# Attention weights made from a second product of keys and queries instead of by transposing, in an attention and mixture-of-experts layer

## The chip, the cores and the metric

The kernel runs on one core of a Trainium2 chip. The metric is the time of one execution on the device in microseconds (us), lower is better. A core has five engines with queues of their own, each executing in order: TensorE (PE, with its weight loads listed as PEld), VectorE (DVE), ScalarE (ACT), GpSimd (POOL) and SyncE (SP), which here only issues DMAs. Matmul results lie in PSUM, which has eight banks of 512 fp32 values for each of 128 partitions.

## The reference

All data is fp32. x is 8 batches x 512 tokens x 256 features.

```python
qkv = x @ w_qkv                       # 16 heads of 16 features
q = q / sqrt(16)
scores = where(causal, q @ k.T, NEG)  # per batch and head, 512 x 512
x = layernorm(x + (softmax(scores) @ v) @ w_out)

probs = softmax(x @ gate_w.T)         # 16 experts
idx = top_k(probs + gate_b, 6)        # the six best for each token
y = sum over chosen e of probs[e] * ((silu(x @ W1.T + B1) * (x @ W3.T + B3)) @ W2.T + B2)   # hidden 176
z = the same form without a gate, hidden 352, for every token (shared expert)
x = layernorm(x + y + z)
```

## The kernel before

**Attention.** A batch's tokens are four blocks of 128 (NT = 4). The 16 heads are eight pairs; heads are reached as m (0 or 1, the half of the features), s (0 or 1, which head of a pair) and r (0 to 3, the group of 32 partitions), so one (m, s) stands for four heads. `transpose_x` brings x to features on partitions, `project_qk` and `project_v` project. Queries are stored once for each s, with the rows of the pair's other head set to zero (`par` holds the parity masks), so that a matmul over 32 partitions gives one head's scores. v is stored in `v2` with 16 columns of ones between the heads, so that the product with v also gives the sum of the weights.

A step is (q, m, s): a block of queries against all keys before it.
- `scores` (L348) makes four matmuls, one for each r, each into a one-bank tile `sc` (the pool ps_s has four such banks). For each, DVE adds the causal mask, scales by -0.25 and takes the minimum in one custom instruction (L368), and POOL forms minimum minus that (L378), that is, the scaled score less its maximum, in `e`.
- `turn_weights` (L384) transposes the 128 x 128 blocks of `e` on PE into a bank of `ps` (L390), and ACT takes the exponential out of it (L392) into `eT`.
- `weighted_v` (L396) multiplies `eT` with v into `po`, whose four r lie in four groups of 32 output columns.
- `normalize` (L407) runs once for each (q, m): ACT and DVE merge the two s, and DVE divides by the sum.

Steps are software-pipelined: unit i holds the scores of step i, the transposes of step i-1 and the product with v of step i-2. There are 16 steps and 18 units a batch.

**Tokens.** After a query block, `later` queues `finish_tokens` (output projection `pr`, residual, norm), `transpose_tokens`, `gate`, `place` and three `send` for it. `gate` and `place` find the six experts of each token and the slots for its row; `send` scatters the rows with indirect DMAs from POOL (L543) to a list of the group in DRAM, `xs`. `shared_units` computes the shared expert of a batch while the next batch's attention runs.

**Experts.** Batches are gathered in GROUPS. When the last row of a group is sent, `table` and `spread` make a list of tiles of 128 rows of one expert. For each tile `expert_units` fetches rows (`xg`, on SP's queue), transposes them (L780) and the hidden layer of an earlier tile (L784), and makes the up product `pab` (L799, bias matmul L806) and the down product `py` (L826); POOL scatters the result to `ys` (L835). `combine_units` loads each token's six rows, sums them with their weights (L893), normalises and stores. A group has 24 tiles for each batch and 15 more: 63, 111 and 63.

**Order.** PE's order is written out by hand (`tc.manual_schedule`); the other engines' queues are ordered by the framework's scheduler. `line` is the list of attention units; `put` spreads the expert units of a group between the units after its last row is sent, until the next group is ready. The units of the last group, and the combine units of the one before among them, run after attention; the combine of the last group runs at the very end, alone. PSUM: four banks ps_s, one ps_o, three ps. In the last group every second tile bank is taken from ps_s.

Of the kernel before, what the change touches and what calls it, by code (L numbers as in the profile page):

```python
# [19 lines left out]
P = 128  # L20
# [3 lines left out]
HD = 16  # L24
TOP_K = 6
NOWHERE = 1 << 20
GROUPS = (2, 4, 2)
# [4 lines left out]
def attn_moe_postln_kernel(  # L32
# [47 lines left out]
    ten = ctx.enter_context(tc.tile_pool(name="ten", bufs=8))  # L80
    dram = ctx.enter_context(tc.tile_pool(name="dram", bufs=1, space=DRAM))
    ps_s = ctx.enter_context(tc.tile_pool(name="ps_s", bufs=4, space=PSUM))
    ps_o = ctx.enter_context(tc.tile_pool(name="ps_o", bufs=1, space=PSUM))
    ps = ctx.enter_context(tc.tile_pool(name="ps", bufs=3, space=PSUM))

# [3 lines left out]
    def load_x(b):  # L89
        t = two.tile([P, NT, E + D], F32, tag="x", name=f"x_{b}")  # L90
        nc.sync.dma_start(out=t[:, :, E:], in_=x[b].rearrange("(t p) d -> p t d", p=P))
        xts[b] = t
# [27 lines left out]
    load_x(1)  # L120

# [19 lines left out]
    none = const.tile([P, E + S], F32, name="none")  # L141
    mask = none[:, E:]
    nc.gpsimd.memset(mask[:, : S - P], 0.0)

    nc.vector.memset(none[:, :E].bitcast(I32), NOWHERE)
    make_causal_mask(nc, mask[:, S - P :], NEG)
# [4 lines left out]
    )  # L151

# [65 lines left out]
    def split_biases():  # L218
# [7 lines left out]
        rest = ten.tile([E, 2, EH], F32, tag="eT", name="rest")  # L226
# [61 lines left out]
    for i in range(2):  # L288
        t = const.tile([P, 3, E], F32, tag=f"vals{i}", name=f"vals{i}")
        nc.gpsimd.tensor_copy(t[:, 1, :], eio)  # L290
        vals.append(t)

    cw = const.tile([P, P], F32, name="cw")
    nc.gpsimd.memset(cw, 0.0)
    nc.gpsimd.memset(cw[:, E : E + 1], 1.0)

    def attention(b):
# [12 lines left out]
        def project_qk(m):  # L310
            xT = st["xT"]
            if m == 0:
                st["qT"] = one.tile([P, ND, 2, S], F32, tag="qT", name=f"qT_{b}")
                st["kT"] = one.tile([P, ND, S], F32, tag="kT", name=f"kT_{b}")
            qT, kT = st["qT"], st["kT"]
            for w in range(2):
# [9 lines left out]
                if w == 0:  # L326
                    nc.scalar.mul(qT[:, m, 0, :], pr, par[:, 0:1])
                    nc.vector.tensor_scalar_mul(qT[:, m, 1, :], pr, par[:, 1:2])
                else:
                    nc.scalar.copy(kT[:, m, :], pr)  # L330
# [17 lines left out]
        def scores(q, m, s):  # L348

            n = (q + 1) * P  # L350
            qT, kT = st["qT"], st["kT"]
            es = []
            nb = four.tile([P, 4], F32, tag="nb", name=f"nb_{b}_{q}_{m}_{s}")
            scs = []
            for r in range(4):
                sc = ps_s.tile([P, S], F32, tag="sc", name=f"sc_{b}_{q}_{m}_{s}_{r}")
                nc.tensor.matmul(  # L357
                    sc[:, :n],
                    lhsT=qT[ts(r, 32), m, s, ts(q, P)],
                    rhs=kT[ts(r, 32), m, :n],  # L360
                    start=True,
                    stop=True,
                )
                scs.append(sc)
            for r in range(4):
                e = eight.tile([P, S], F32, tag="e", name=f"e_{b}_{q}_{m}_{s}_{r}")

                nc.vector.tensor_tensor_reduce(  # L368
                    out=e[:, :n],
                    in0=scs[r][:, :n],  # L370
                    in1=mask[:, S - n :],
                    scale=-0.25,
                    scalar=BIG,
                    op0=ALU.add,
                    op1=ALU.min,
                    accum_out=nb[:, r : r + 1],
                )
                nc.gpsimd.tensor_scalar(  # L378
                    e[:, :n], e[:, :n], -1.0, nb[:, r : r + 1], ALU.mult, ALU.add
                )  # L380
                es.append(e)
            return es

        def turn_weights(q, m, s, es):  # L384

            eTs = []
            for k in range(q + 1):
                tp = ps.tile([P, S], F32, tag="ps", name=f"tp_{b}_{q}_{m}_{s}_{k}")
                for r in range(4):
                    nc.tensor.transpose(tp[:, ts(r, P)], es[r][:, ts(k, P)], ident)  # L390
                eT = ten.tile([P, S], F32, tag="eT", name=f"eT_{b}_{q}_{m}_{s}_{k}")
                nc.scalar.activation(eT, tp, AF.Exp)  # L392
                eTs.append(eT)
            return eTs

        def weighted_v(q, m, s, eTs, po):  # L396
            for k in range(q + 1):
                for r in range(4):
                    nc.tensor.matmul(  # L399
                        po[ts(r, 32), m, s, :],  # L400
                        lhsT=v2[:, k, 4 * m + r, s : s + 2, :].rearrange("p h i -> p (h i)"),
                        rhs=eTs[k][:, ts(r, P)],
                        start=(k == 0),
                        stop=(k == q),
                    )

        def normalize(q, m, po, aT):  # L407

            nm = f"{b}_{q}_{m}"
            po = po[:, m]  # L410
            t = []
            for i in range(2):
                a = two.tile([P, P], F32, tag=f"t{i}", name=f"t{i}_{nm}")
                nc.scalar.mul(a, po[:, i, :], par[:, 1:2])
                t.append(a)
            den = two.tile([P, P], F32, tag="den", name=f"den_{nm}")

            nc.vector.scalar_tensor_tensor(
                t[0], po[:, 1, :], par[:, 0:1], t[0], ALU.mult, ALU.add
            )  # L420
            nc.vector.stream_shuffle(den, t[0], SWAP)
            nc.vector.reciprocal(den, den)
            nc.vector.scalar_tensor_tensor(  # L423
                t[1], po[:, 0, :], par[:, 0:1], t[1], ALU.mult, ALU.add
            )
            nc.vector.tensor_mul(aT[:, m, :], t[1], den)

        def finish_tokens(t, aT):
            pr = ps.tile([P, D], F32, tag="ps", name=f"pr_{b}_{t}")
            for c in range(ND):  # L430
                nc.tensor.matmul(
                    pr,
                    lhsT=aT[:, c, :],
# [16 lines left out]
        def gate(t):  # L450
# [17 lines left out]
            v = vals[t % 2]  # L468
# [14 lines left out]
            rank = two.tile(shp, F32, tag="rank", name=f"rank_{nm}")  # L483
            nc.vector.tensor_reduce(rank, gt, AX.X, ALU.add)
            sel = two.tile(shp, F32, tag="sel", name=f"sel_{nm}")
            nc.vector.tensor_scalar(sel, rank, TOP_K - 0.5, None, ALU.is_lt)
            nc.vector.tensor_mul(cw[:, :E], sel, pb)
            st["gate", t] = rank, sel

        def place(t):  # L490

            nm = f"{b}_{t}"
            rank, sel = st.pop(("gate", t))
            v = vals[t % 2]
# [38 lines left out]
            idi = two.tile([P, TOP_K], I32, tag="idi", name=f"idi_{nm}")  # L533
# [22 lines left out]
        steps = [(q, m, s) for q in range(NT) for m in range(ND) for s in range(2)]  # L556
        done = {}

        def front(i):

            if i < len(steps):
                done[i] = scores(*steps[i])
            if 1 <= i <= len(steps):
                done[i - 1] = turn_weights(*steps[i - 1], done[i - 1])
# [467 lines left out]
```

## Time and profile before

| what | value |
|---|---|
| median of 11 runs | 1595.69 us (1593.44 to 1599.05) |
| the profiled execution | 1594.6 us, of which the span is 1592.9 us |
| mean granted TensorE clock | 0.936 |
| busy: PE, DVE, ACT, POOL | 1401.8, 849.2, 619.5, 814.2 us |
| transposes of the weights (L390) | 1280 matmuls, 200.9 us |
| subtraction on POOL (L378) | 512 instructions, 271.8 us |

A line of a group gives the source line, the engine and operation, the written and read tiles, the shape and the count; then busy time, mean duration in ns, and idle time of the engine ahead of it with what ended it. A line of a timeline has the start in us, the duration of the merged run, engine, line, operation, tiles and count. A line of a table by windows has the stretch, its length, each engine's busy time with the count of instructions, and at the end the granted clock (1.00 is full speed), the busy share of the DMA engines and GB/s. Matmuls overlap and their ends are modelled, so distances between starts tell more than durations. An fp32 matmul shows as two records, an fp32 transpose as one.

### The profile page before, as it was taken

How to read it: one execution, taken by the hardware profiler on the slowest of the kernel's cores; microseconds unless marked ns; L12 is line 12 of the kernel's file. 1: busy time of each engine (PE TensorE's matmuls, PEld its weight loads, DVE VectorE, ACT ScalarE, POOL GpSimd, SP SyncE). 2: the span in 40 equal slices, each digit the busy share in tenths (PEclk: the TensorE clock that was granted, in tenths of full speed). 3: DMA queues.
4: the chain of work that ended last, by engine and by line, in shares of the span. 5: the costliest groups of instructions: out<-in, count | busy, mean ns of one | idle time of the engine just before them, and what ended most of it. 6: DMA issues, size and time to landing. Idle time of an engine off the chain costs nothing.

```text
span 1592.9 us, 30354 instructions
## 1 busy us (share of the span) xinstructions
PE 1401.8 (88%) x9204; PEld 950.9 (60%) x9204; DVE 849.2 (53%) x3058; ACT 619.5 (39%) x1637; POOL 814.2 (51%) x1127
## 2 busy tenths in 40 slices
PE   7698998999998899899999899998998998889950
PEld 4464664665765567566656666666665666556730
DVE  4565756755655564566466634455443332774235
ACT  2243333343443334344343444444443443334520
POOL 4367566657465454746565446534645422443320
PEclk9897988998999999899999999999999999999985
DMA  9711112221121121212221325222243523785334
GB/s 263 208 43 43 49 37 94 62 66 62 57 69 56 45 63 52 73 41 68 76 88 56 110 82 147 78 86 78 75 121 109 159 69 85 229 237 147 96 89 132
DMA packets 147497, 151.37 MB, mean 95 GB/s; under 512 B 51215, under 2 KB 122499, under 8 KB 147338
## 3 DMA queue, kind: packets, MB, share of 16 engines
q1 hardware_dynamic: 126474, 96.69, 22.3%
q0 software_dynamic: 20592, 51.96, 9.0%
q8 instruction: 78, 1.28, 0.3%
q14 instruction: 81, 0.66, 0.1%
q10 hardware_dynamic: 272, 0.79, 0.1%
HBM read 75.61 MB, written 79.58 MB: 97 GB/s over the span
## 4 chain that ended last, share of the span: by engine, by line
PE 65%; DVE 12%; POOL 9%; DMA 6%; issue 5%; ACT 2%; SPq 0%; POOLq 0%; DVEq 0%; ACTq 0%
PE pab L799 15%; PE py L826 10%; PE tp L390 8%; PE sc L357 5%; PE po L399 4%; PE qk L319 4%; PE pa L603 3%; DVE e L368 3%; POOL e L378 3%; PE tb L780 2%; PE tb L784 2%; PE pb L603 2%; PE spy L629 2%; POOL xs L543 2%; DVE o L893 2%
## 5 line engine op out<-in xcount | busy, mean ns | idle before, releaser
L835 POOL DMA_INDIRECT ys<-y,yat x237 | 239.2, 1009 | 307.0 <-ACT y L834 264.2
L799 PE MATMUL pab<-we_sb,xgT 128*128 x936 | 336.5, 483 | 12.9 <-DVE h L817 9.8
L378 POOL TENSOR_SCALAR e<-e,nb 128x512 f32<-128x512 f32 (+3 forms) x512 | 271.8, 542 | 140.7 <-DVE nb L368 127.9
L392 ACT ACTIVATE eT<-tp 128x512 f32<-128x512 f32 x320 | 173.3, 599 | 269.3 <-PE tp L390 268.9
L826 PE MATMUL py<-we_sb,hT 88*128 x948 | 247.3, 383 | 12.4 <-ACT hT L791 5.6
L368 DVE CUSTOM_DVE_ANT_0 e<-sc,none 128x512 f32<-128x512 f32 (+3 forms) x512 | 228.1, 478 | 42.2 <-PE sc L357 40.6
L390 PE MATMUL tp<-ident,e 128*128 128x128 f32 x1280 | 200.9, 301 | 47.8 <-POOL e L378 44.6
L543 POOL DMA_INDIRECT xs<-x,idi x192 | 189.7, 988 | 77.0 <-issue 42.2
L390 PEld LDWEIGHTS tp<-ident,e 128*128 128x128 f32 x1280 | 152.0, 150 | 124.9 <-POOL e L378 76.7
L826 PEld LDWEIGHTS py<-we_sb,hT 88*128 88x128 f32 x948 | 171.3, 192 | 79.7 <-issue 45.8
L816 DVE SCALAR_TENSOR_TENSOR h<-h,pab 128x176 f32<-128x176 f32 x237 | 79.2, 334 | 256.4 <-ACT h L815 255.8
L799 PEld LDWEIGHTS pab<-we_sb,xgT 128*128 128x128 f32 x936 | 164.7, 196 | 83.3 <-issue 12.9
L815 ACT ACTIVATE h<-pab 128x176 f32<-128x176 f32 x237 | 75.2, 317 | 197.0 <-PE pab L806 197.0
L357 PE MATMUL sc<-kT,qT 32*128 32x384 f32 (+3 forms) x1024 | 137.0, 500 | 14.7 <-DVE nb L368 14.4
L834 ACT COPY y<-py 128x256 f32<-128x256 f32 x237 | 88.2, 372 | 146.6 <-PE py L826 145.5
L787 ACT COPY xgT<-tb 128x256 f32<-128x256 f32 x234 | 87.1, 372 | 105.0 <-PE tb L784 83.8
L893 DVE SCALAR_TENSOR_TENSOR o<-yg,kept,o 128x256 f32<-128x256 f32 x192 | 94.3, 491 | 43.5 <-DMA o<-acc 23.7
L784 PE MATMUL tb<-ident,h 128*88 128x128 f32 x474 | 93.2, 279 | 20.4 <-DVE h L817 20.3
L399 PE MATMUL po<-eT,v 128*32 128x128 f32 x2560 | 99.1, 283 | 1.2 <-DVE t L423 1.2
L780 PE MATMUL tb<-ident,xg 128*128 128x128 f32 x468 | 92.6, 279 | 6.0 <-issue 4.5
L357 PEld LDWEIGHTS sc<-kT,qT 32*128 32x128 f32 x1024 | 58.2, 192 | 54.2 <-DVE nb L368 28.4
L791 ACT COPY hT<-tb 88x256 f32<-88x256 f32 x237 | 88.1, 372 | 5.6 <-PE tb L784 5.6
(161 smaller groups left out, 1713.3 us busy)
## 6 DMA issues: line engine op xcount, KB each, us to landing
xg<-xs SPq DMA_DIRECT2D x237, 128.0 KB
yg<-ys SPq DMA_DIRECT2D x96, 256.0 KB
we_sb<-in_w SPq DMA_DIRECT2D x6, 1408.0 KB
xs<-none SPq DMA_DIRECT2D x3, 2176.0 KB
xs<-none SPq DMA_DIRECT2D x48, 136.0 KB
x<-in_x SPq DMA_DIRECT2D x8, 512.0 KB
acc<-x SPq DMA_DIRECT2D x32, 128.0 KB
o<-acc SPq DMA_DIRECT2D x32, 128.0 KB
```

The source lines that it names most:

```text
L357: nc.tensor.matmul(sc[:, :n], lhsT=qT[ts(r, 32), m, s, ts(q, P)], rhs=kT[ts(r, 32), m, :n], start=True, stop=True,)
L368: nc.vector.tensor_tensor_reduce(out=e[:, :n], in0=scs[r][:, :n], in1=mask[:, S - n :], scale=-0.25, scalar=BIG, op0=ALU.add, op1=ALU.min, ...
L378: nc.gpsimd.tensor_scalar(e[:, :n], e[:, :n], -1.0, nb[:, r : r + 1], ALU.mult, ALU.add)
L390: nc.tensor.transpose(tp[:, ts(r, P)], es[r][:, ts(k, P)], ident)
L392: nc.scalar.activation(eT, tp, AF.Exp)
L399: nc.tensor.matmul(po[ts(r, 32), m, s, :], lhsT=v2[:, k, 4 * m + r, s : s + 2, :].rearrange("p h i -> p (h i)"), rhs=eTs[k][:, ts(r, P)], ...
L543: d = nc.gpsimd.indirect_dma_start(out=grp.xs, out_offset=bass.IndirectOffsetOnAxis(ap=idi[:, k : k + 1], axis=0), in_=xts[b][:, t, :], in ...
L784: nc.tensor.transpose(tp[:HC, 2 + c, :], h[:, ts(c, HC)], ident)
L799: nc.tensor.matmul(pab, lhsT=xgT[:, c, :], rhs=we_sb[:, ds(e * WE + c * 2 * EH, 2 * EH)], start=(c == 0), stop=False,)
L826: nc.tensor.matmul(py, lhsT=hT[:, c, :], rhs=we_sb[:HC, ds(e * WE + 4 * EH + c * D, D)], start=(c == 0), stop=(c == 1),)
L835: d = nc.gpsimd.indirect_dma_start(out=grp.ys, out_offset=bass.IndirectOffsetOnAxis(ap=st["at", j].bitcast(I32), axis=0), in_=y, in_offset ...
L893: nc.vector.scalar_tensor_tensor(o, y, kept[b][:, t, k : k + 1], o, ALU.mult, ALU.add)
```

## The change

The weights are no longer transposed. A piece is now a third of an (m, s), and three pieces make up all four query blocks of it; a batch has 12 pieces.

- `scores(m, s, f)` makes the products with queries on partitions into one tile of four banks, all four r in it. DVE adds the mask to the diagonal blocks in place in PSUM, and one reduction for each query block writes the negative maximum of four heads to `top`. Nothing else is kept of these scores.
- `subtract(m, s)` transposes `top` for the four query blocks and adds it to the query tile, in one row of each head's 32 that the zeroed other head leaves free. The key tile has a row of ones there (`row`), so that a product of keys and queries comes out less the maximum.
- `weights(m, s, f)` makes the products a second time, with keys on partitions, in a tile of the same pool; DVE adds the mask `maskT` to the diagonal blocks, and ACT takes the exponential of up to 2048 columns in one instruction into `eT`.
- `sums(m, s, f)` multiplies with v: a matmul covers all query blocks of a key block (512 to 128 columns), 16 for each (m, s). Merging and dividing by the sums is done on 512 columns for each m, the shuffle, reciprocal and product still for 128.
- The pools: `ps_s` has one tile of four banks that `scores` and `weights` share; key tiles exist once for each s. The pool of eight `eT` becomes one of two tiles of four times the size. After attention, `ps_s` and `ps_o` are closed and five banks `ps2` are opened, which tiles use in turn with `ps`.
- The order: a piece is two entries of `line`, first scores of piece p and sums of piece p-4, then weights of piece p-3 (and `subtract` after the third piece). The token steps of a batch follow its last piece, one block an entry, and so its 24 scatters come within six entries; its shared units follow them.
- GROUPS is (1, 4, 3), so tiles are 39, 111 and 87. x is loaded three batches ahead instead of two: the third load is issued on SP ahead of the expert weights.

```diff
-GROUPS = (2, 4, 2)
+GROUPS = (1, 4, 3)
...
-    ps_s = ctx.enter_context(tc.tile_pool(name="ps_s", bufs=4, space=PSUM))
+    ps_s = attention_banks.enter_context(tc.tile_pool(name="ps_s", bufs=1, space=PSUM))
...
     load_x(1)
+    load_x(2)
...
+                    if w == 1:
+                        nc.scalar.activation(
+                            t, pr, AF.Identity, bias=row[:, i : i + 1], scale=par[:, i : i + 1]
+                        )
...
+        def scores(m, s, f):
+            qT, kT = st["q", m, s], st["k", m, s]
+            sc = ps_s.tile([P, 4, S], F32, tag="sc", name=f"sc_{b}_{m}_{s}_{f}")
+            blocks = ((0, 0), (1, P)) if f == 0 else ((f + 1, 0),)
+            for q, at in blocks:
                 for r in range(4):
                     nc.tensor.matmul(
+                        sc[:, r, at : at + (q + 1) * P],
+                        lhsT=qT[ts(r, 32), ts(q, P)],
+                        rhs=kT[ts(r, 32), : (q + 1) * P],
...
+            for q, at in blocks:
+                last = sc[:, :, at + q * P : at + (q + 1) * P]
+                nc.vector.tensor_tensor(
+                    last, last, mask.unsqueeze(1).to_broadcast([P, 4, P]), ALU.add
+                )
+                nc.vector.tensor_reduce(
+                    top[:, q, HD - HD * s :: 2 * HD],
+                    sc[:, :, at : at + (q + 1) * P],
+                    AX.X, ALU.max, negate=True,
+                )
+        def subtract(m, s):
+            qT = st["q", m, s]
+            tp = ps.tile([P, S], F32, tag="ps", name=f"top_{b}_{m}_{s}")
+            for q in range(NT):
+                nc.tensor.transpose(tp[:, ts(q, P)], top[:, q, :], ident)
+            nc.vector.scalar_tensor_tensor(
+                qT, tp, row[:, s : s + 1], qT, ALU.mult, ALU.add
+            )
+        turned = (((0, 0),), ((1, 0), (3, S - P)), ((2, 0),))
+        def weights(m, s, f):
+            qT, kT = st["q", m, s], st["k", m, s]
+            sc = ps_s.tile([P, 4, S], F32, tag="sc", name=f"st_{b}_{m}_{s}_{f}")
+            for k, at in turned[f]:
+                for r in range(4):
+                    nc.tensor.matmul(
+                        sc[:, r, at : at + S - k * P],
+                        lhsT=kT[ts(r, 32), ts(k, P)],
+                        rhs=qT[ts(r, 32), k * P :],
...
+            nc.vector.tensor_tensor(
+                first, first,
+                maskT.unsqueeze(1).unsqueeze(1).to_broadcast([P, 4, len(turned[f]), P]),
+                ALU.add,
+            )
+            n = sum(S - k * P for k, _ in turned[f])
+            eT = two.tile([P, 4, S], F32, tag="eT", name=f"eT_{b}_{m}_{s}_{f}")
+            nc.scalar.activation(eT[:, :, :n], sc[:, :, :n], AF.Exp, scale=0.25)
...
+        def sums(m, s, f):
...
+                        po[ts(r, 32), k * P :],
                         lhsT=v2[:, k, 4 * m + r, s : s + 2, :].rearrange("p h i -> p (h i)"),
+                        rhs=eT[:, r, at : at + S - k * P],
...
+    def first_half(p):
+        part(p, "scores")
+        part(p - 4, "sums")
+        if p - 4 >= 0 and (p - 4) % pieces == pieces - 1 and p - 4 < total:
+            parts[(p - 4) // pieces].finish()
...
+    def second_half(p):
+        part(p - 3, "weights")
+        if p < total and p % 3 == 2:
+            part(p, "subtract")
...
+    for p in range(total + 4):
+        line.append(lambda p=p: first_half(p))
+        line.append(lambda p=p: second_half(p))
```

## The prediction

> **What bounds the kernel now.** I read the page first. PE is the engine that is busy almost throughout, and the chain that ended last runs through it for two thirds of the span; the change takes its third line (`tp`, 8% of the span) and POOL's 272 us of `e` away.
>
> ```profile
> PE 1401.8 (88%) x9204; PEld 950.9 (60%) x9204; DVE 849.2 (53%) x3058; ACT 619.5 (39%) x1637; POOL 814.2 (51%) x1127
> PE 65%; DVE 12%; POOL 9%; DMA 6%; issue 5%; ACT 2%; SPq 0%; POOLq 0%; DVEq 0%; ACTq 0%
> ```
>
> A share over the whole span hides the stages, so I cut it at the first `qk` of each batch (105, 213, 328, 469, 617, 761, 920 us), at the end of batch 7's attention and at the last `ys` scatter. The columns are PE, PEld, DVE, ACT and POOL busy, then granted clock and DMA.
>
> ```profile
> 0.00:105.00 105.00, 81.20 (x652) 53.05 (x656) 57.65 (x233) 34.08 (x73) 50.72 (x104) 0.89 0.65 187
> 105.00:213.00 108.00, 98.07 (x776) 64.89 (x772) 69.32 (x275) 38.46 (x86) 69.00 (x104) 0.87 0.13 44
> 213.00:328.00 115.00, 105.26 (x812) 69.10 (x800) 75.36 (x302) 41.46 (x95) 70.83 (x106) 0.87 0.20 67
> 328.00:920.00 592.00, 546.91 (x3965) 366.82 (x3956) 338.86 (x1265) 243.15 (x620) 345.49 (x487) 0.96 0.22 66
> 920.00:1225.00 305.00, 286.60 (x1733) 197.20 (x1723) 142.71 (x509) 131.70 (x373) 156.62 (x197) 0.98 0.33 97
> 1225.00:1536.00 311.00, 283.73 (x1307) 199.86 (x1305) 133.38 (x395) 130.70 (x390) 116.44 (x123) 0.99 0.47 135
> 1536.00:1593.00 57.00, 0.00 (x0) 0.00 (x0) 31.94 (x81) 0.00 (x0) 5.08 (x8) 0.54 0.49 145
> ```
>
> Counted by the bias matmul (one for each tile), 69 expert tiles lie in the fourth row, 70 in the fifth, 95 in the sixth. The clock is low where attention runs without tiles.
>
> The timeline of PE gives the cost of each burst as the distance of starts, which the modelled ends blur.
>
> ```profile
> 284.39 0.86 PE L399 MATMUL po<-eT,v 128*32 128x128 f32 x24
> 285.18 0.93 PE L357 MATMUL sc<-kT,qT 32*128 32x384 f32 x8
> 286.04 1.53 PE L390 MATMUL tp<-ident,e 128*128 128x128 f32 x12
> 291.25 1.14 PE L357 MATMUL sc<-kT,qT 32*128 32x512 f32 x8
> 292.32 1.53 PE L390 MATMUL tp<-ident,e 128*128 128x128 f32 x12
> ```
>
> Four score matmuls (8 records) take 0.86 us at 384 columns and 1.07 at 512; at 128 and 256 the same distances are 0.43 and 0.64. Twelve transposes take 1.40 (0.117 each), three blocks of `po` 0.79. An expert tile at full rate starts every 2.81 us (`py` at 1234.39, 1237.20, 1240.02).
>
> **PE's floor before and after.** Call the four query blocks of one (m, s) pair a quad; a batch has four. A quad costs PE now: scores 0.43 + 0.64 + 0.86 + 1.07 = 3.0, 40 transposes x 0.117 = 4.7, `po` 0.36 + 0.58 + 0.79 + 1.01 = 2.7; 10.4 us. The change removes the 4.7, adds the scores a second time with the same column counts (3.0) and four transposes of `top` with a switch (0.6), and does `po` in 16 matmuls in place of 40 over the same columns, about 2.9 by the score rows. That is 9.5, so PE gains only 0.9 us a quad. Everything else of a batch stays: qk 7.3, v 3.5, xp 1.0, `pr` 3.6, x1 1.0, gate 1.8, place 3.2, shared 10.3 + 7.3 = 39 us. Floors: 81 us a batch before, 77 after, 29 us in all. Tiles stay 237 (63 + 111 + 63 becomes 39 + 111 + 87).
>
> Against floors, the stages now take 108 / 81 = 1.33 (alone), 592 / (4 x 81 + 69 x 2.81 = 518) = 1.14 (mixed), 305 / 278 = 1.10 (dense), 311 / (267 + 20) = 1.08 (tail). These losses are what the change can win or add to.
>
> **The new chain.** `sc` goes from four one-bank buffers to one four-bank buffer, used in turn by `scores` and by the `weights` of three pieces earlier. So in each piece (three make a quad): scores on PE, mask and maximum on DVE, weights on PE, mask on DVE, exp on ACT, and only then the next scores. PE executes in order, so `sums`, projections, token steps and tiles queued behind the next `scores` wait with it, and with them ACT's copies `xgT`, `hT`, `y` and DVE's `h`. Rows for its steps:
>
> ```profile
> L368 DVE CUSTOM_DVE_ANT_0 e<-sc,none 128x512 f32<-128x512 f32 x128 | 82.4, 677 | 6.5 <-PE sc L357 6.4
> L392 ACT ACTIVATE eT<-tp 128x512 f32<-128x512 f32 x320 | 173.3, 599 | 269.3 <-PE tp L390 268.9
> L640 DVE TENSOR_TENSOR x<-spy,x 128x256 f32<-128x256 f32 x32 | 13.5, 421 | 28.9 <-PE spy L636 28.9
> L484 DVE TENSOR_REDUCE rank<-gt 128x16 f32<-128x256 f32 x32 | 13.4, 420 | 48.1 <-POOL gt L482 48.0
> L529 DVE TENSOR_REDUCE kp<-all 128x18 f32<-128x288 f32 x32 | 14.5, 454 | 34.7 <-POOL all L525 34.7
> ```
>
> The reduce rows give 1.06 ns an element and 0.15 us: 0.69, 1.24, 1.78, 2.32 us for 512, 1024, 1536, 2048. An add that writes PSUM in place does not occur in the trace; L640 reads PSUM at about the same slope, so 512 is 0.69 and 1024 1.22. Its bounds are 0.42 (the 256-wide row) and 0.95 (a 128-wide reciprocal, the slowest row); I take 0.69, which is nearest in kind. Copies on ACT of 128, 256 and 512 columns take 268, 372 and 585 to 599 ns, hence 0.83 ns an element and 1.87 us for 2048. By piece:
> - first: 1.07 + (4 DVE operations, 3.3) + 1.07 + 0.69 + 1.87 = 8.0, less 0.5 since the first mask needs only the first four matmuls: 7.5;
> - second: 0.86 + 2.47 + 1.29 + 1.22 + 1.87 = 7.7;
> - third: 1.07 + 3.0 + 0.64 + 0.69 + 1.03 = 6.4.
>
> With five handovers a piece of about 0.07 us (from the 0.05 to 0.1 between releaser and start in the timeline) a quad is 22.7 us, a batch 91. PE's part of that is 6; the rest are two gaps a piece, 2.5 to 3.3 us after the scores and 1.7 to 3.1 after the weights, to be filled with 39 us a batch and the tiles.
>
> DVE rises too. Now it does 270 / 32 = 8.4 us a quad for the maxima; then 6.0 for reduces, 2.8 and 2.6 for the two masks and 0.75 for `subtract` (a 512-wide operation from PSUM): 12.1, so 15 us a batch more. Less 2.5 us a batch for the wider `t`, its total is 84 + 12 = 96 a batch (the 84 being its rows of attention, gate and shared, 668 us over 8 batches). POOL loses 272 us, which is on the path only through the waits of `tp` (45 on PE, 77 on PEld); what is late next is the DVE reduce. ACT is about even. The 24 scatters of a batch now come in six items, 24 x 1.3 = 31 us of POOL; the `all` of the last block and the norms queue behind, which tiles hide except at the last group. The third x load goes ahead of the expert weights on SP: 0.5 MB at 187 GB/s, under 3 us, felt at most by the 11.3 us that DVE waits in split_biases.
>
> **Two rules weighed.** In the trace the four-bank evacuation would cost DVE and ACT 11.4 and 4.8 us a quad against 6 us of matmuls, so by rows alone the read-out is the longer part. The Trainium skill, TensorEngine Tiling (Array Packing), section PSUM Bottleneck, says that tiling speeds TensorE but not the reading of PSUM, which may become the bottleneck; that speaks against the change, as the rows do.
>
> ```profile
> 120.00:124.00 4.00, 3.26 (x19) 2.28 (x18) 2.68 (x20) 1.12 (x3) 3.26 (x8) 1.00 0.01 2
> 124.00:128.00 4.00, 3.57 (x20) 2.73 (x20) 1.83 (x16) 0.65 (x2) 3.31 (x6) 0.50 0.09 35
> ```
>
> Here the clock halves though no row shows PE idle for long. The Trainium skill, TensorE: Matmul & The Clock Gate, Part 1, has the half clock follow an idle window of about 3.4 us; by that, gaps of 3 us would leave the clock at 1.0 and batch 1 at some 116 us, where the rows make me take 120.
>
> **The sum by stage.**
> - Batch 0: 12 us of loads, transposes and qk, 12 for the first three pieces, which have no weights, 3 x 22.7, and the 11 of split_biases: 103.
> - Batch 1, alone: DVE 96, chain 91, PE 77, each waiting for the others in order. Before, the largest was 84 (DVE) and it took 108 (1.29); 1.25 x 96 = 120, as POOL's queue no longer stands between, 0.04 of it for the clock.
> - Batches 2 to 5, 39 tiles: PE 77 + 27 = 104, DVE 102, chain 91. At 0.43 tile units an item, more than half of the gaps hold none and stay at 2.5 to 3 us, while a gap with a tile and another unit has 5 to 6 us of PE. Before 1.14 with four buffers; I take 1.21, 126 each, 504.
> - Batches 6 and 7, 77 tiles: 154 + 216 = 370, gaps full; the 1.9 us exp can hold up an `hT` copy: 1.09, 403.
> - Tail, 121 tiles: 340 + 29 for batch 7's end = 369, x 1.08 = 399.
> - The last combine is exposed and has 12 token tiles in place of 8. Pairs start 11.2 to 11.4 us apart:
>
> ```profile
> 1539.77 3.09 DVE L893 SCALAR_TENSOR_TENSOR o<-yg,kept,o 128x256 f32<-128x256 f32 x6 [3.58 <-DMA yg<-ys]
> 1550.96 3.09 DVE L893 SCALAR_TENSOR_TENSOR o<-yg,kept,o 128x256 f32<-128x256 f32 x6 [1.66 <-DMA o<-acc]
> ```
>
> 57 + 4 x 5.7 = 80.
>
> Sum 103 + 120 + 504 + 403 + 399 + 80 = 1609, and 1.7 around the span (1594.6 against 1592.9) makes 1611. The median lies 1.1 above the profiled execution: 1612.
>
> **Rivals.**
> - Faster: PE stays fed in batches 1 to 5. Price: mixed at 1.12 (117 each), batch 1 at 1.16 (110), dense and tail at 1.05 (389, 388): 103 + 110 + 468 + 389 + 388 + 80 + 3 = 1541. It decides where a mixed quad falls under 30.5 us (forecast 31.5; 16 us over 16 quads). For it: POOL's waits go; DVE has slack in tiles. Against: one buffer.
> - Slower still: half clock in batches 0 to 5. PE's 6 us in the chain becomes 12 for about half of the quads, 24 x 3 = 72: 1684. For it: the clock of 0.87 above; against: PE busier per piece with tiles.
> - The PSUM add at 0.95 costs 0.26 for each of 8 blocks of 512 a quad, over 24 quads 50 us (1662); at 0.42 it gains as much (1562). Both ends lie in the range.
> - The group sizes alone do it: 23 us on the last combine, 1619 with attention unchanged; not told apart by the time, but by the stages.
>
> **How the numbers follow.** Forecast 0.45 (its own range is 1590 to 1640: 0.02 faster, 0.05 the same, 0.38 slower), fed PE 0.35, slower cases 0.20. About 0.2% (3 us) is what a measurement of this kernel can tell from no change: faster 0.37, same 0.05, slower 0.58. The range reaches to both rivals, 1540 to 1684, and takes in both ends of the PSUM add.
>
> **What would show it.** Right: `sc` at `scores` waiting for ACT `eT` and PE waiting for the DVE reduce as the largest waits of PE in batches 0 to 5; DVE near 949 us, POOL near 540; batch starts 120 to 128 us apart; 80 us after the last scatter. Wrong: batches 2 to 5 near 115 us with PE over 95% busy, or a clock under 0.8 there.

## Result and profile after

The changed kernel takes 1836.2 us (median of 8 runs, 1833.7 to 1839.5); the kernel before, run beside it, 1596.5 (31 runs). The ratio is 1.151, 95% interval 1.149 to 1.152. The forecast was 1612 us with 1540 to 1684 as its range, so the sign was right and the size missed by 224 us. The profiled execution took 1835.6 us with a span of 1833.9.

The page's busy line and its chain that ended last, to be read beside those of before:

```profile
PE 1416.4 (77%) x7540; PEld 837.8 (46%) x7540; DVE 975.3 (53%) x2324; ACT 588.3 (32%) x1333; POOL 543.8 (30%) x623
PE 15%; DMA 5%; DVE 3%; POOL 2%; issue 1%; ACT 1%; SPq 0%; POOLq 0%; DVEq 0%; ACTq 0%
```

No engine did much more than forecast (DVE 975 where 949 was said, POOL 544 where 540 was said), PE does about as much as before, and its idle time grew from 191 to 418 us. The second line covers only the end of the span (its shares sum to 27%), so the stages have to tell where the time went. Busy time of PE, PEld, DVE, ACT and POOL, then clock and DMA, cut at the first `qk` of batches 1, 2 and 6 and at the last `ys` scatter:

```profile
0.00:97.00 97.00, 53.52 (x303) 24.30 (x303) 39.61 (x55) 19.45 (x21) 6.73 (x34) 0.70 0.70 198
97.00:249.00 152.00, 99.03 (x528) 46.14 (x532) 87.16 (x195) 35.13 (x48) 35.17 (x40) 0.70 0.11 37
249.00:892.00 643.00, 488.54 (x2737) 262.53 (x2738) 372.73 (x825) 189.18 (x346) 178.92 (x198) 0.84 0.14 45
1754.00:1834.00 80.00, 0.00 (x0) 0.00 (x0) 47.74 (x120) 0.00 (x0) 7.61 (x12) 0.51 0.53 154
```

Against the sum by stage: batch 0 took 97 (forecast 103), batch 1 152 (120), batches 2 to 5 643 (504), everything from batch 6 to the last `ys` 862 (802), the last combine 80 (80). In batch 1 PE is busy 65% of the time and DVE 57%; neither is the bound.

From the view of waits, the waits of PE, DVE and ACT at the score tile, and DVE's two for POOL's part of the gate (us in total, times, longest):

```profile
ACT eT L445 <- DVE st L437: 238.1, 80, 11.7
DVE sc L397 <- PE sc L388: 141.8, 76, 4.3
PE sc L388 <- ACT eT L445: 133.2, 47, 9.5
DVE rank L540 <- POOL gt L538: 104.6, 22, 8.6
DVE kp L586 <- POOL all L582: 64.9, 21, 6.6
PE st L428 <- DVE top L400: 35.5, 22, 3.1
```

The first three and the last are the new chain, as forecast. The other two were there before (48 and 35 us) and have about doubled. The timeline shows what such a wait does (start, duration, engine, line):

```profile
206.27 0.95 POOL L600 DMA_INDIRECT xs<-x,idi  x1 [0.31 <-issue]
207.24 0.74 POOL L537 TENSOR_TENSOR eq<-eq,lower 128x256 f32<-128x256 f32 x1
208.15 1.01 POOL L600 DMA_INDIRECT xs<-x,idi  x1 [0.17 <-issue]
209.19 0.73 POOL L538 TENSOR_TENSOR gt<-gt,eq 128x256 f32<-128x256 f32 x1
209.95 0.42 DVE L540 TENSOR_REDUCE rank<-gt 128x16 f32<-128x256 f32 x1 [5.65 <-POOL gt L538]
210.29 0.69 DVE L437 TENSOR_TENSOR st<-st,maskT 128x512 f32<-128x512 f32 x1
211.01 1.88 ACT L445 ACTIVATE eT<-st 128x2048 f32<-128x2048 f32 x1 [4.87 <-DVE st L437]
212.94 1.66 PE L388 MATMUL sc<-k,q 32*128 32x384 f32 x8 [6.43 <-ACT eT L445]
```

POOL's two short operations stand between row scatters of 1 us each. DVE, in order, waits 5.65 us for them with the mask of the weights queued behind, although PE had finished those weights at 204.6; ACT waits 4.87, and PE, whose next instruction is the next `scores`, 6.43.

And a stretch of batch 1 with nothing of POOL and little else in it (PE, DVE and ACT):

```profile
126.59 1.66 PE L388 MATMUL sc<-k,q 32*128 32x128 f32 x16 [0.88 <-ACT eT L445]
128.39 0.70 DVE L397 TENSOR_TENSOR sc<-sc,mask 128x512 f32<-128x512 f32 x1 [1.89 <-PE sc L388]
129.13 0.69 DVE L400 TENSOR_REDUCE top<-sc 128x4 f32<-128x512 f32 x1
129.85 0.70 DVE L397 TENSOR_TENSOR sc<-sc,mask 128x512 f32<-128x512 f32 x1
130.59 1.23 DVE L400 TENSOR_REDUCE top<-sc 128x4 f32<-128x1024 f32 x1
131.96 2.09 PE L428 MATMUL st<-q,k 32*128 32x512 f32 x8 [2.69 <-DVE top L400]
134.11 0.70 DVE L437 TENSOR_TENSOR st<-st,maskT 128x512 f32<-128x512 f32 x1 [2.29 <-PE st L428]
134.90 1.88 ACT L445 ACTIVATE eT<-st 128x2048 f32<-128x2048 f32 x1 [4.30 <-DVE st L437]
```

The windows' row of the same time:

```profile
127.00:137.00 10.00, 4.53 (x36) 1.45 (x33) 4.02 (x5) 3.14 (x3) 0.00 (x0) 0.50 0.00 0
```

This is one piece of the bare chain. Every step hands over within 0.15 us, the clock (the number after POOL's) is 0.50, the first mask starts only after all eight score matmuls (16 records), and four matmuls of 512 columns take 2.15 us to the start of their mask, not 1.07. The three pieces from 118.04 to 145.74, a quad, take 27.7 us.

### The profile page after: what moved, and what is told of

It reads as the page before. It is cut to its first block, busy times and chain, and to the rows that moved or that the text cites. A ratio compares the mean times of both kernels' runs of the same rounds, so it can differ in the third digit from the quotient of the medians.

```text
span 1833.9 us, 24868 instructions
## 1 busy us (share of the span) xinstructions
PE 1416.4 (77%) x7540; PEld 837.8 (46%) x7540; DVE 975.3 (53%) x2324; ACT 588.3 (32%) x1333; POOL 543.8 (30%) x623
## 5 line engine op out<-in xcount | busy, mean ns | idle before, releaser
L871 PE MATMUL py<-we_sb,hT 88*128 x948 | 257.1, 394 | 33.3 <-ACT hT L836 21.9
L388 PE MATMUL sc<-k,q 32*128 32x128 f32 (+3 forms) x1024 | 123.9, 584 | 140.4 <-ACT eT L445 133.2
L445 ACT ACTIVATE eT<-st 128x2048 f32<-128x2048 f32 (+1 forms) x96 | 153.0, 1593 | 238.2 <-DVE st L437 238.1
L600 POOL DMA_INDIRECT xs<-x,idi x192 | 189.3, 986 | 83.0 <-issue 40.8
L400 DVE TENSOR_REDUCE top<-sc 128x4 f32<-128x512 f32 (+3 forms) x128 | 190.6, 1489 | 2.9
L397 DVE TENSOR_TENSOR sc<-sc,mask 128x512 f32<-128x512 f32 x128 | 89.0, 696 | 142.2 <-PE sc L388 141.8
L428 PE MATMUL st<-q,k 32*128 32x512 f32 (+3 forms) x1024 | 107.5, 514 | 57.9 <-DVE top L400 35.5
L388 PEld LDWEIGHTS sc<-k,q 32*128 32x128 f32 x1024 | 45.3, 223 | 179.3 <-ACT eT L445 153.4
L437 DVE TENSOR_TENSOR st<-st,maskT 128x512 f32<-128x512 f32 (+1 forms) x96 | 83.8, 873 | 62.9 <-PE st L428 62.7
L455 PE MATMUL po<-eT,v 128*32 128x512 f32 (+3 forms) x1024 | 115.9, 557 | 0.0
L279 POOL TENSOR_TENSOR rstd_a<-mv_a,nhalf 128x1 f32<-128x1 f32 x32 | 19.3, 604 | 325.1 <-DVE mv_a L278 315.6
```

What stands on the lines that cost most here:

```text
L388: nc.tensor.matmul(sc[:, r, at : at + (q + 1) * P], lhsT=qT[ts(r, 32), ts(q, P)], rhs=kT[ts(r, 32), : (q + 1) * P], start=True, stop=True,)
L400: nc.vector.tensor_reduce(top[:, q, HD - HD * s :: 2 * HD], sc[:, :, at : at + (q + 1) * P], AX.X, ALU.max, negate=True,)
L428: nc.tensor.matmul(sc[:, r, at : at + S - k * P], lhsT=kT[ts(r, 32), ts(k, P)], rhs=qT[ts(r, 32), k * P :], start=True, stop=True,)
L445: nc.scalar.activation(eT[:, :, :n], sc[:, :, :n], AF.Exp, scale=0.25)
L455: nc.tensor.matmul(po[ts(r, 32), k * P :], lhsT=v2[:, k, 4 * m + r, s : s + 2, :].rearrange("p h i -> p (h i)"), rhs=eT[:, r, at : at + S ...
L600: d = nc.gpsimd.indirect_dma_start(out=grp.xs, out_offset=bass.IndirectOffsetOnAxis(ap=idi[:, k : k + 1], axis=0), in_=xts[b][:, t, :], in ...
```

## Experiments

Four theories are named in the expectations. **Theory 1**: one score tile used in turn, with engines that work in order, so that a wait on any of them stops all. **Theory 2**: the half clock. **Theory 3**: DVE has too much work in the chain. **Theory 4**: the group sizes. The runs were made on several chips, on which the kernel before took from 1592 to 1661 us; between chips only ratios to it are compared. Intervals are 95%. Even the ratio may carry over only roughly. Where the kernel before took 1650 us (half_gate, gate_pe_mask, before_gate, before_groups_143) or 1661 us (spread_late, before_late, gate_no_recip, gate_pe_mask_242), DVE waits some 31 to 66 us in all for nothing that the profile shows ("issue"), against 0 to 8 us in the other runs, where the kernel before took 1592 to 1597. So a difference of one or two hundredths in the ratio between the two sets is not shown.

**Two tiles of half the size (half_buffers).** `sc` becomes two tiles of two banks with two heads each, for scores and for weights.

```diff
-ps_s = ... bufs=1      sc = ps_s.tile([P, 4, S], ...)
+ps_s = ... bufs=2      scs = [ps_s.tile([P, 2, S], ...) for h in range(2)]
```

> The changed kernel with the one four-bank score tile cut into two tiles of two banks (heads r 0, 1 and r 2, 3), so that one half can be read by DVE or ACT while the other is written. DVE has 11 more operations a quad, at 0.15 us each 53 us in all. Theory 1 (one tile used in turn, each link waiting in an in-order queue, sets the pace of batches 0 to 5; a piece takes 13.4 us there where its links add up to 7.6): a piece falls to about 11, so 1836 - 72 x 2.4 = about 1660. Theory 2 (the half clock alone is the price): 1800 to 1836, since the clock stays low. Theory 3 (DVE has too much work): slower, 1850 to 1890.

Measured 1802.0 us, ratio 1.130 (1.126 to 1.135). That is 34 us under the changed kernel, far less than theory 1 expected: splitting the tile alone does not free the chain.

**The gate's POOL operations on DVE (gate_on_dve).**

```diff
-nc.gpsimd.tensor_mul(eq, eq, lower)
-nc.gpsimd.tensor_add(gt, gt, eq)
+nc.vector.tensor_mul(eq, eq, lower)
+nc.vector.tensor_add(gt, gt, eq)
...
-nc.gpsimd.tensor_mul(all3, ...)
+nc.vector.tensor_mul(all3, ...)
```

> The changed kernel with the three POOL operations of gate and place (two products of 128 x 256, one of 128 x 288) moved to DVE, so that DVE no longer waits in the middle of its queue for POOL, whose queue holds the scatters. DVE gets 32 x (2 x 0.42 + 0.45) = 41 us more work and loses 170 us of waits (rank 105, kp 65). Theory 1 with in-order waits: these waits hold up masks and reduces of the one score tile; 1836 falls by 60 to 120, to about 1745. Theory 2 (clock): about 1830. Theory 3 (DVE work): 1850 to 1880.

Measured 1719.6 us, ratio 1.078 (1.068 to 1.089): 116 us less (110 and 124 in its two runs), though DVE does 30 us more. The waits of `rank` and `kp` are gone. Its stages (batch 1, batches 2 to 5, batch 6 to the last `ys`):

```profile
96.00:231.00 135.00, 94.72 (x533) 44.31 (x532) 90.93 (x207) 35.25 (x48) 24.84 (x27) 0.71 0.11 38
231.00:819.00 588.00, 476.12 (x2724) 257.62 (x2728) 387.61 (x872) 189.05 (x346) 142.14 (x152) 0.87 0.16 50
819.00:1644.00 825.00, 761.84 (x3986) 499.06 (x3983) 439.23 (x1167) 343.97 (x918) 289.50 (x304) 0.97 0.35 103
```

17, 55 and 37 us less than in the changed kernel. The edit also takes 72 us of work off POOL. But what else DVE waits for POOL, the two `rstd` of the norms, is 40 us in both kernels, and PE waits under 3 us for fetched rows in either: `rank` and `kp` are the only waits for POOL that went. Batches 2 to 5 are still at 147 us each, where 126 was forecast.

**A warmer clock (warm).** Unused matmuls in each entry of `line`, two up to entry 47 and one up to 143.

```diff
+for c in range(2 if i < 48 else 1):
+    nc.tensor.matmul(wt, lhsT=ident, rhs=wqkv_sb[:, 0, :S], start=True, stop=True)
```

> The changed kernel with matmuls added that nothing uses: at each of the first 48 entries of the order two, at entries 48 to 143 one, each a 128 x 512 fp32 product of 0.85 us at full clock, behind all else of the entry, so that PE works where it waited. 192 of them, 163 us of PE. Theory 2 (clock): the clock of batches 0 to 5 goes from 0.70 to 0.86 up to 0.95 or more, PE's part of each piece falls by about 1 us in 72 pieces, less what overflows: 1770 to 1810. Theory 1: the gaps are set by DVE and ACT; 1830 to 1880, with the clock up.

Measured 1840.0 us, ratio 1.154 (1.149 to 1.159), at a mean clock of 0.924 in place of 0.860. In batch 1 the clock is 0.94 in place of 0.70 and the stage 147 us in place of 152; theory 2 had expected 1770 to 1810. The clock that is won pays for the work that holds it up, and no more. But the trace shows what the half clock costs the bare chain. These are the starts of the same quad as above, now at a clock of 1.00:

```profile
119.58 1.14 PE L388 MATMUL sc<-k,q 32*128 32x512 f32 x8 [1.41 <-ACT eT L445]
143.78 1.14 PE L388 MATMUL sc<-k,q 32*128 32x512 f32 x8 [1.41 <-ACT eT L445]
```

24.2 us in place of 27.7: the half clock is 3.5 us of a bare quad.

**The groups (after_groups_242 and before_groups_143).** First the changed kernel with `GROUPS = (2, 4, 2)`, then the kernel before with `(1, 4, 3)`.

> The changed kernel with the group sizes of the kernel before, (2, 4, 2) in place of (1, 4, 3). If the groups were the loss it would come near 1600. By the other theories it moves little: the last combine is 23 us shorter (8 token tiles in place of 12), and the tail has 24 fewer tiles (67 us), which move into the batches, where gaps are empty early on and full late: 1770 to 1830.

> The kernel before, with GROUPS = (1, 4, 3) in place of (2, 4, 2) and nothing else changed. If the group sizes cost what the last combine and the shorter mixed part make of it (theory 4, 28 us by the kernel after run with the old groups), this is 1593 + 25 to 30 = about 1620. If in the kernel after the 28 us came from an interaction with the single score tile (39 tiles instead of 69 beside batches 2 to 5, so fewer fillers), this is only the 23 us of the last combine, or less.

Measured 1807.7, ratio 1.134 (1.125 to 1.142), and 1685.8 beside 1649.8, ratio 1.022 (1.019 to 1.025). The groups cost 28 us in the changed kernel and 36 in the kernel before; the forecast had 23.

**Halves and gate together (half_gate).** The first two edits in one kernel.

> The kernel after with the gate's three POOL operations on DVE and the one four-bank score tile as two two-bank tiles used in turn. Theory 1 (the one tile is the loss, only hidden so far by DVE's waits for POOL): the halves now overlap, 1650 to 1670, i.e. 50 to 70 under the gate alone (1720). Theory 3 (what is left is DVE's work and its order, which the halves do not lessen, and which has 350 more instructions here): 1690 to 1720.

Measured 1794.7 beside 1649.8, ratio 1.088 (1.079 to 1.096): nothing is won over the gate alone. PE waits 57 us for `eT` at `scores`, half as long as with the gate alone (120 us):

```profile
PE sc L391 <- ACT eT L450: 57.3, 35, 6.4
```

Yet the time does not fall. That the sharing of one tile is by itself the price is not borne out, though two tiles of half the size, with 24 us more of DVE's work, are not the second full tile that would test it.

**Masks on TensorE (gate_pe_mask).** The gate on DVE, and the masks accumulated by a bf16 identity in place of DVE's two adds.

```diff
-nc.vector.tensor_tensor(last, last, mask..., ALU.add)
+nc.tensor.matmul(sc[:, r, at + q * P : at + (q + 1) * P], lhsT=identb, rhs=mask, start=False, stop=True)
```

> The kernel after with the gate's three POOL operations on DVE and both masks added by TensorE (bf16 identity times mask, accumulated into the score banks) instead of by VectorE in place; oh is one buffer for space. It takes 5.4 us a quad (172 us in all) from DVE and from the chain, and puts 32 matmuls of 128 columns a quad on PE. Theory 3 (DVE's share of the chain sets the pace): 24 quads of batches 0 to 5 lose 4 us each, 96 us, to about 1625. Theory 2 / PE order (PE's own queue sets the pace): the added matmuls cost as much as they save, 1700 to 1740.

Measured 1740.4 beside 1649.8, ratio 1.055 (1.041 to 1.069), 0.024 under the gate alone, some 38 us at 1594, though the intervals overlap and the two runs are from different chips. By that figure, taking 172 us of masks out of DVE and the chain brought less than half of the 96 expected.

**Later reduces (spread_late and before_late).** No work changes its engine: DVE's reduces of `gt` and `all3` are issued one entry after POOL's operations, first in the changed kernel (with the token steps two entries apart, since `eq` and `all3` share a buffer), then in the kernel before.

```diff
-later(4 + t, lambda t=t: gate(t))
-later(6 + t, lambda t=t: place(t))
+later(5 + 2 * t, lambda t=t: gate(t))
+later(6 + 2 * t, lambda t=t: ranks(t))    # the reduce of gt, and sel, cw
+later(6 + 2 * t, lambda t=t: place(t))
+later(7 + 2 * t, lambda t=t: pick(t))     # the reduce of all3, and idi
```

> The kernel after with no work moved between engines: the token steps of a batch come two entries apart instead of one, and DVE's reduces of gt (rank) and all3 (kp) are issued one entry after POOL's operations that they read. If DVE's in-order wait for POOL is what costs (theory 1: gate_on_dve won 0.072 of the ratio), the waits of rank and kp fall from 105 and 65 us to under 20 each and the ratio from 1.151 to about 1.08 (1.07 to 1.10). If gate_on_dve won because POOL had less to do and the scatters went out sooner, this stays above 1.12.

> The kernel before, in which DVE's reduces of gt (rank) and all3 (kp) are issued one entry after POOL's operations; nothing else is moved. In its profile DVE waited 48 and 35 us there; moving the POOL operations to DVE gave a ratio of 0.992 at 35 us more DVE work. If the wait was the price, this gives 0.98 to 0.992; if it was POOL's load (its e operations queue behind), 0.995 to 1.005.

The first gave 1.113 (1.098 to 1.128), less than expected. Its waits say why: an entry is not long enough for `gt`.

```profile
DVE rank L546 <- POOL gt L538: 76.3, 29, 6.2
DVE kp L597 <- POOL all L588: 17.4, 21, 1.3
```

76 us of wait went, and 0.037 of the ratio, some 60 us; in gate_on_dve 170 us went and 116 us were won. Both put the price of a us of this wait near 0.7 to 0.8 us, the first within a wide interval, on another chip and with the token steps moved as well. The kernel before with later reduces gave 1.001 (0.999 to 1.004). That says little of the wait's price there, since the edit left most of the wait in place (48 and 35 us before):

```profile
DVE rank L490 <- POOL gt L482: 35.4, 26, 4.2
DVE kp L540 <- POOL all L531: 32.4, 26, 2.3
```

**The gate on DVE in the kernel before (before_gate).** The same three lines.

> The kernel before with only the gate's three POOL operations moved to DVE. In its profile DVE waits 48 us for gt and 35 us for all on POOL; if these waits are on the path as in the kernel after, where moving them won 116 us, this wins 20 to 60 us (1535 to 1575) and is faster than both kernels. If four score buffers ride over them, it stays within 10 us of 1593.

Measured 1636.3 beside 1649.8, ratio 0.992 (0.989 to 0.995): 0.8% faster than the kernel before. Here both waits are gone, 83 us by the profile of before, and 13 us were won: about 0.16 us for a us of wait if all of it is the wait's, where the changed kernel gave 0.7. Whether the 13 us come from the wait or from POOL's shorter queue, with `e` in it, was not shown apart.

**No reciprocal (gate_no_recip).**

```diff
-nc.vector.reciprocal(den[:, cols], den[:, cols])
```

> The kernel with the gate's operations on DVE, and the reciprocal of the softmax sums left out (the attention output stays unnormalised): it takes 64 operations of 0.9 us, some 60 us, from DVE alone. Theory 3 (DVE's own work stands in the chain, so each us of it is paid): the ratio falls from 1.078 by 0.02 to 0.04. If PE's order sets the pace, it falls by under 0.01.

Ratio 1.069 (1.062 to 1.076): 60 us of DVE's work are worth 0.009, some 15 us, within the intervals of nothing and from another chip. It fits a DVE whose gaps take operations of 0.9 us off the chain, where waits of 5 us cost; it does not show it.

**Masks on TensorE with the old groups (gate_pe_mask_242).**

> The kernel with the gate on DVE and the masks added by TensorE, and the old groups (2, 4, 2). If the three prices found so far simply add, the ratio is 1.055 - 0.020 = 1.035 (1.025 to 1.045), about 55 us above the kernel before, which then is the price of the chain itself. If the groups' price came only from too few tiles beside a slow chain, less is won: 1.045 to 1.055.

Ratio 1.039 (1.029 to 1.048): inside the range for prices that add; the other range, from 1.045, is not quite excluded.

**The price of a us of chain (gate_exp_twice and gate_copy_after).** With the gate on DVE, exp done twice from the score banks, and as a control the same ACT work after the banks are free.

```diff
 nc.scalar.activation(eT[:, :, :n], sc[:, :, :n], AF.Exp, scale=0.25)
+nc.scalar.activation(eT[:, :, :n], sc[:, :, :n], AF.Exp, scale=0.25)    # gate_exp_twice
+nc.scalar.copy(eT[:, :, :n], eT[:, :, :n])                              # gate_copy_after
```

> The kernel with the gate's operations on DVE, and each exp done twice from the score banks into the same eT: 1.59 us on the mean are added to the chain of each of 96 pieces, and to ACT. If the chain is the path in all pieces, the time grows by 96 x 1.59 = 153 us (ratio 1.078 + 0.096 = 1.17); if it is the path in batches 0 to 5 alone, by 72 x 1.59 = 114 (1.15). If PE's and DVE's own order set the pace and the chain has slack, by under 40 us (under 1.10).

> The control to gate_exp_twice: after each exp, ACT copies eT onto itself, about the same ACT time, but the score banks are free for the next scores when exp ends, so the chain is not longer. The difference to gate_exp_twice is the price of the chain: nearly all of that kernel's excess by the chain theory (this one then at 1.08 to 1.10), none if it was ACT's load.

Measured 1874.0, ratio 1.177 (1.174 to 1.180), and 1805.4, ratio 1.134 (1.132 to 1.136). The excess over the gate alone is 154 us, what a chain that is the path in every piece must give; but the control has 86 us of it. So 68 us are what the longer chain adds over the control. The other 86 come with 155 us of copies, although ACT is busy only 41% of the time there. They need not be ACT's own order: the control is not wholly off PE's path, since `sums` reads `eT` and waits for the copy, which no `po` of the gate alone did. PE's waits for `eT` in the first, and in the control at `scores` and at `sums`:

```profile
PE sc L388 <- ACT eT L446: 207.8, 57, 8.6
...
PE sc L388 <- ACT eT L445: 118.7, 47, 7.0
PEld po L456 <- ACT eT L446: 67.6, 55, 1.7
PE po L456 <- ACT eT L446: 19.4, 33, 1.1
```

**Shorter tile units (gate_split).** With the gate on DVE, `down` of a tile becomes a unit of its own.

```diff
     up(j)
-    down(j - 2)
 units.append(unit)
+units.append(lambda j=j: down(j - 2))
```

> The kernel with the gate on DVE, where the second half of each tile unit (the two py matmuls, their copy and the ys scatter) is a unit of its own, so that the units between two steps of the chain are half as long and twice as many. If PE's units are longer than the chain's gaps (weights start 1.7 us after the maxima in batches 2 to 5), this wins 30 to 60 us (ratio 1.04 to 1.06). If the chain alone sets the pace, nothing: 1.07 to 1.085.

Measured 1686.4, ratio 1.059 (1.057 to 1.062): 33 us won by order alone. Batches 2 to 5 take 562 us (234 to 796) in place of 588. This is what units longer than the chain's gaps would give; that more and smaller units are also spread more evenly was not tested apart.

**Two more versions of the kernel before, and everything together.** The gate on DVE and groups (3, 4, 1) in the kernel before; the same with shorter units; and the changed attention with the gate on DVE, masks on TensorE, shorter units and groups (3, 4, 1).

> The kernel before with the gate's POOL operations on DVE and groups (3, 4, 1). The exposed last combine falls from 8 to 4 token tiles, 4 x 5.7 = 23 us less, against fewer tiles beside batch 2, which then runs alone (115 us in the profile of before with few tiles, against 141 with 17). If the group sizes act through the last combine, 0.992 - 0.014 = 0.978; if the tiles moved out of the mixed part cost as much, 0.99 to 1.0.

> The kernel before with the gate on DVE, groups (3, 4, 1) and the tile units in two halves. If the shorter units help because a chain with one score tile has short gaps, nothing changes here, where four score buffers let PE run ahead: 0.968 to 0.978 (0.972 without the halves). If they help PE's order in any kernel, 0.95 to 0.965.

> The changed attention with everything that the runs found to cost taken away: gate on DVE, masks added by TensorE, tile units in two halves, groups (3, 4, 1). If the prices add: 1.078 - 0.024 (masks) - 0.020 (units) - 0.034 (groups, as on the kernel before) = 1.000 (0.99 to 1.01). If the chain leaves a price of its own, more than half of it in the batches without tiles, which are now three: 1.01 to 1.03.

Measured 1548.3 us, ratio 0.972 (0.971 to 0.974); 1547.9, ratio 0.971 (0.967 to 0.974); 1598.3, ratio 1.004 (1.002 to 1.005). The shorter units do nothing in the kernel with four buffers. The changed attention, with every price found taken away, comes within 0.4% of the kernel before but not to the better versions of it: 50 us stay. Busy lines of the changed attention at its best and of the shorter-unit kernel:

```profile
PE 1407.6 (88%) x8564; PEld 853.1 (53%) x8564; DVE 834.7 (52%) x2197; ACT 590.1 (37%) x1333; POOL 472.7 (30%) x527
...
PE 1400.3 (91%) x9204; PEld 946.4 (61%) x9204; DVE 891.6 (58%) x3154; ACT 618.5 (40%) x1637; POOL 752.5 (49%) x1031
```

PE's work differs by 7 us, its idle time by 42 (1595.1 - 1407.6 against 1545.6 - 1400.3). So most of what stays is PE waiting, not PE working; which of the remaining links it waits for was not taken apart.

## Why the prediction was right or wrong

**Right.** The durations: the in-place PSUM add 0.69 to 0.70 (taken as 0.69), the four reduces 0.69, 1.22, 1.76 and 2.29, the exp 1.88. The engines' totals to 3%, the exposed combine at 80 us, the waits of PE that were named. The read-out is longer than the matmuls: 11.4 us of DVE a quad, as the rows said.

**Wrong: the bare chain, 22.7 us a quad.** It measured 27.7 in batch 1. Between the start of scores and of the mask, the three pieces took 1.80, 1.80 and 2.22 us, 5.8 in all, where the forecast had 2.5 and three handovers, 2.7: 3.1 too little. 0.5 of it is the deduction for a first mask that starts after four matmuls; it waited for all eight. From weights to their mask it was 1.30, 2.15 and 1.21, 4.7 against 3.2, another 1.5. Most of the rest is the half clock, which the forecast put at 4 us for the whole of batch 1: at a clock of 1.00 (warm) the same quad takes 24.2, so 3.5 of the 5.0 us missed are the clock and 1.5 the deduction and the handovers. The Trainium skill, TensorE: Matmul & The Clock Gate, Part 1, has the half clock follow an idle window of about 3.4 us; here PE's longest wait between 117 and 137 us was 3.31 and the clock 0.50. So the forecast's reading of that rule, that gaps of 3 us leave the clock at 1.0, failed, and its own row of 124 to 128 us, with a clock of 0.50 and PE 3.57 of 4 us busy, was the better guide. With 27.7 a quad the chain, not DVE, is the longest part of batch 1 (111 us), and 111 plus the forecast's own 24 us of overhead is 135. Batch 1 takes 135 without POOL's waits, but the 24 us were a factor on DVE's work, so that the two agree proves nothing; no run took them apart.

**Wrong: POOL's burst, "which tiles hide except at the last group".** This is the largest error, 116 of 224 us. The forecast counted 31 us of scatters on POOL as hidden and named who queues behind on POOL, but not that DVE waits in order for `gt` and `all3` between them, with the chain's masks behind DVE. "POOL's queue no longer stands between" was true of `e` alone. gate_on_dve shows what stood in its place: 170 us of DVE's waits, worth 116 us. before_gate shows that the price is new: the same edit won 13 us in the kernel before.

**Wrong: mixed batches at 1.21.** Without POOL's waits they took 147 us each, not 126. The forecast let tiles fill the gaps; it did not charge for tiles longer than the gaps. gate_split won 26 us of these four batches back, 6 a batch; the longer bare chain would be up to 20 a batch more (an estimate, 4 x 5.0 us; it was not measured in these batches). Of the 60 us missed after batch 5, 37 went with POOL's waits in gate_on_dve; the other 23 were not taken apart.

**The rivals.** The fed PE (1541) fell with its one condition, a quad under 30.5 us; the mixed quad took 40 (643 / 16). The half clock was real; it was priced at 6 us for half of the quads, and in the bare chain it cost 3.5. The PSUM add at other prices did not occur. The groups alone are 28 to 36 us, more than the 23 forecast. No rival had the wait of one engine on another in the middle of the chain, and so the range was too narrow.

## What to carry to other kernels

When several buffers used by a chain of engines become one, expect in-order waits on any of those engines to move onto the path: list for each link not only its duration but the waits of the instructions queued ahead of it, the small bookkeeping ones that cost little before included. A us of such a wait was worth about 0.7 us here and about 0.16 in the kernel with four buffers. That the buffers make this difference is argued, not shown: the two kernels differ in more, in how close together the scatters come among other things, and no run gave the new chain a second full tile. Work that is to fill a chain's gaps should come in small pieces: halving the tile units won 33 us here and nothing in the kernel before.

## What the hardware showed that was not expected

- TensorE's granted clock stayed at 0.50 from 117 to 137 us with PE waits of 0.9 to 3.3 us between its bursts and PE busy 11.2 of the 20 us. Raising the mean from 0.860 to 0.924 by unused matmuls left the time as it was (1836 and 1840 us).
- A row scatter occupies POOL for 0.99 us on the mean (189.3 us in 192), more than the 0.73 us of the operations between which it stands; in the wait of 5.65 us shown above, POOL did three whole ones and the end of a fourth.
- An engine busy for 41% of the span can still cost: 155 us of copies on ACT, which the score tile does not wait for, made the kernel 86 us longer; PE's `sums` did wait for them, by how much of the 86 is open.
